# Flamingo layer 0 on one core: the first loads in three groups, and the first maxima on VectorE in a fixed order

## The chip, the core and the metric

The kernel runs on one core of a Trainium2 chip. TensorE (PE) multiplies and transposes, VectorE (DVE), ScalarE (ACT) and GpSimd (POOL) do the rest, and SyncE (SP) issues transfers; ACT and POOL issue transfers too. Each engine works through its own list of instructions in order. The metric is the device time of one execution in microseconds (us).

## The reference

Two layers, each a gated cross-attention-like block and a gated feed-forward block, over `x` of 4 batches of 512 rows by 512:

```python
x = x + tanh(g_xattn[0]) * L0_xattn(layernorm(x), fside, ctx)   # int8 "smooth quant" expert, per batch
x = x + tanh(g_ffn[0])   * L0_ffn(layernorm(x), w_fc, w_proj)   # ternary weights
x = x + tanh(g_xattn[1]) * L1_xattn(layernorm(x), ctx, mask, Wq, Wk, Wv, Wo)   # 16 heads, 8 of keys/values
x = x + tanh(g_ffn[1])   * L1_ffn(layernorm(x), router_w, norm_w, gate_w, up_w, down_w)   # top 2 of 8 experts

def smooth_quant_linear(x, w):          # fside (512 x 512), then ctx (512 x 256), are its weights
    s = sqrt(max(amax_cols(|x|), eps) / max(amax_cols(|w|), eps))
    xq, wq = int8 rounding of x / s and w * s, with a scale per row
    return xq @ wq.T * x_scale * w_scale.T

def ternarize(w):                       # w_fc 1280 x 512 and w_proj 512 x 1280
    m = mean(|w|);  return m * (sign of w where |w| > 0.7 m, else 0)
```

The keys and values of layer 1, `ctx @ Wk` and `ctx @ Wv`, depend on no earlier layer.

## The kernel before

Layer 0 runs batch by batch. `int8_block(b)` normalises `X[b]` (`layer_norm`: statistics on VectorE, a root on ScalarE, four normalisations on ScalarE, line 180). It takes the column maximum of the weight `fside` (`weight_max`: one VectorE reduction, line 259, four transposes on PE, line 264, and a small tail) and those of the normalised rows (`column_max`: per 128 columns four transposes, line 198, and a reduction, line 251). From both come the factors: `up_q` (line 294), its root (`sqrt_of`, lines 151 to 158), and two rows made by transposes (line 204). ScalarE copies one row out (line 300); VectorE divides the rows (line 303) and GpSimd multiplies the weight (line 305). Then row maxima (275), scaling (281), transposed copies to bf16 on ScalarE (283), the products (336), `h` (340), SiLU (341), and the same again with the 256 columns of `ctx` as the weight (`cr`).

`mean_of` adds up absolute values of the two ternary weights on ScalarE (line 395). `w_fc` is held in ten tiles (`hold_rows`), while `w_proj` comes through two staging buffers of tag `t8` (`stage_rows`, line 368). `load_signs` turns both into signs on VectorE (414, 417). `ternary_in` and `ternary_block(b)` are the ternary feed-forward (462, 449).

`keys_values(b)` makes the keys and values of layer 1 ahead of time and fills gaps of PE with them: the context is transposed (495) and copied (496), then 16 products of two matmuls (501) per batch. ScalarE copies each product (503) into one of two staging slots, and SP stores it to DRAM (504). A copy therefore needs the store of two products earlier to have landed. The products use two PSUM banks in turn.

The code is written batch by batch, and a scheduler puts the instructions of each engine in order by priority, which is the order of the code unless `tc.high_priority` says otherwise, and by its own estimate of when things are ready. `tc.keep_in_program_order` pins an instruction, and `tc.add_manual_dep` adds a dependency. What an engine has in its list is fixed before the run.

In the kernel before, the loads at the start are issued without waiting: SP issues `x[0]`, `fside[0]`, the cross rows `cr` and the context of batch 1; ACT issues the context of batch 0, `Wk` and `Wv`; POOL issues the gates and `fside[1]`. The loads of `w_fc` alone have a dependency on `Wv`:

```python
        fs0, cr0 = load_rows(0), load_cross(0)
        ctx0 = load_context(0, nc.scalar)
        ...
        held = hold_rows(w_fc)
        fs1 = load_rows(1, nc.gpsimd)
```

Layer 1 follows: attention over 64 heads in a software pipeline, and the experts.

Of the kernel before, what the change touches and what calls it, by code (L numbers as in the profile page):

```python
# [15 lines left out]
P = 128  # L16
# [41 lines left out]
def kernel(  # L58
# [82 lines left out]
    def acc_tile():  # L141
        sums_in[0] += 1
        return bank(4 + sums_in[0] % 4)

    def small(n, tag):
        return sm.tile([P, n], F32, tag=tag, name=tag)

# [62 lines left out]
    with tc.tile_pool(name="q8", bufs=1) as q8, tc.tile_pool(name="l0", bufs=2) as l0, tc.tile_pool(  # L210
# [29 lines left out]
        def home():  # L240
            mine = HOMES[now[0]]
            return bank(mine[next_of("home", len(mine))])
# [5 lines left out]
        def column_max(src, kt, dst):  # L248

            for i in range(kt):  # L250
                nc.vector.tensor_reduce(
                    dst[:, i : i + 1], transposed(src, i, home()), AX.X, ALU.max, apply_absolute_value=True
                )

        def weight_max(w, kt, tag):

            k = kt * P
            top = rooms[now[0]][0]
            nc.vector.tensor_reduce(
                top[:, :k], w.rearrange("p t k -> p k t"), AX.X, ALU.max, apply_absolute_value=True  # L260
            )
            tp = home()
            for i in range(kt):
                nc.tensor.transpose(tp[:, i * P : (i + 1) * P], top[:, i * P : (i + 1) * P], ident)
            am = q8.tile([P, kt], F32, tag=tag + "_am", name=tag + "_am", bufs=2)
            nc.vector.tensor_reduce(am, tp[:, :k].rearrange("p (k t) -> p k t", t=P), AX.X, ALU.max)
            nc.vector.tensor_scalar_max(am, am, Q_EPS)
            nc.vector.reciprocal(am, am)
            return am

        def quantize(src, kt, dst, tag):
# [12 lines left out]

            return sc

        def smooth_quant(a, w, w_max, kt, tag):


            k = kt * P  # L290
            am = small(kt, tag + "_am")
            column_max(a, kt, am)
            q = small(kt, tag + "_q")
            nc.vector.scalar_tensor_tensor(q, am, Q_EPS, w_max, ALU.max, ALU.mult)
            s = sqrt_of(q, kt, tag + "_s")
            nc.vector.tensor_scalar_max(s, s, Q_EPS)
            rs = small(kt, tag + "_rs")
            nc.vector.reciprocal(rs, s)
            s_row = a_row()
            nc.scalar.copy(s_row[:, :k], row_of(s, kt, home())[:, :k])  # L300
            rs_row = row_of(rs, kt, home())
            for t in range(NT):
                nc.vector.tensor_tensor(a[:, t, :], a[:, t, :], rs_row[:, :k], ALU.mult)
            for t in range(NT):
                nc.gpsimd.tensor_tensor(w[:, t, :], w[:, t, :], s_row[:, :k], ALU.mult)
            aT = q8.tile([P, kt, S], BF16, tag=f"q{kt}", name="aT", bufs=2)
            wT = q8.tile([P, kt, S], BF16, tag=f"q{kt}", name="wT", bufs=2)
            a_sc = quantize(a, kt, aT, tag + "a")
            w_sc = quantize(w, kt, wT, tag + "w")
            w_row = a_row()  # L310
            nc.scalar.copy(w_row, row_of(w_sc, NT, home()))
            return aT, wT, a_sc, w_row

        def load_rows(b, queue=nc.sync):
            fs = row_tiles(b % 2 * 2)
            queue.dma_start(fs, rows(fside[b]))
            if b:
                queue.dma_start(X[b], rows(x[b]))
            return fs

        def load_cross(b):
            cr = place_in(dn, SLOT + 3072, NT * DC).rearrange("p (t k) -> p t k", t=NT)
            nc.sync.dma_start(cr, rows(cvec[b]))
            return cr

        def int8_block(b, fs, cr):
            now[0] = b
            xn = row_tiles(b % 2 * 2 + 1)
            layer_norm(b, xn)
            fs_max = weight_max(fs, KD, "fs")  # L330
            aT, wT, a_sc, w_row = smooth_quant(xn, fs, fs_max, KD, "up")
            act = xn[:, : NT // 2, :].rearrange("p a (b n) -> p (a b) n", n=INNER)
            for t in range(NT):
                ps = home()
                for i in range(KD):
                    nc.tensor.matmul(
                        ps, lhsT=aT[:, i, t * P : (t + 1) * P], rhs=wT[:, i, :], start=(i == 0), stop=(i == KD - 1)
                    )
                h = l0.tile([P, 512], F32, tag="h", name="h")
                nc.vector.scalar_tensor_tensor(h, ps, a_sc[:, t : t + 1], w_row, ALU.mult, ALU.mult)  # L340
                nc.scalar.activation(act[:, t, :], h[:, :INNER], AF.Silu)
                nc.gpsimd.tensor_tensor(act[:, t, :], act[:, t, :], h[:, INNER:], ALU.mult)
            cr_max = weight_max(cr, INNER // P, "cr")
            aT, wT, a_sc, w_row = smooth_quant(act, cr, cr_max, INNER // P, "dn")
            gsc = small(NT, "gsc")
            nc.vector.tensor_scalar(gsc, a_sc, tg_xa0, None, ALU.mult)
            for t in range(NT):
                ps = home()
                for i in range(INNER // P):
                    nc.tensor.matmul(  # L350
                        ps,
                        lhsT=aT[:, i, t * P : (t + 1) * P],
                        rhs=wT[:, i, :],
                        start=(i == 0),
                        stop=(i == INNER // P - 1),
                    )
                y = l0.tile([P, 512], F32, tag="h", name="y")
                nc.vector.scalar_tensor_tensor(y, ps, gsc[:, t : t + 1], w_row, ALU.mult, ALU.mult)
                nc.gpsimd.tensor_tensor(X[b][:, t, :], X[b][:, t, :], y, ALU.add)
# [5 lines left out]

        def stage_rows(src, r, n_cols):
            st = l0.tile([P, HF], F32, tag="t8", name="stage")
            nc.gpsimd.dma_start(st[:, : n_cols * P], src[r * P : (r + 1) * P, :])
            return st[:, : n_cols * P]

        def hold_rows(src):

            loads = [nc.gpsimd.dma_start(X[2], rows(src[: NT * P, :]))]
            held = [X[2][:, r, :] for r in range(NT)]
            for r in range(NT, NH):
                held.append(l0.tile([P, D], F32, tag="hT", name="held", bufs=6))
                loads.append(nc.gpsimd.dma_start(held[-1], src[r * P : (r + 1) * P, :]))
            for load in loads:
                tc.add_manual_dep(
                    load.ins,  # L380
                    wkv_in[-1].ins.name,
                    mybir.DependencyInfo(mybir.DependencyClass.Sync, mybir.DependencyReason.DATA),
                    reason="what the first products read comes first",
                )
            return held

        def mean_of(src, n_rows, n_cols, tag, held=None):

            part = small(n_rows + 1, tag + "_part")
            for r in range(n_rows):  # L390
                if held:
                    st, dst = held[r], l0.tile([P, D], F32, tag="r", name="size")
                else:
                    st = dst = stage_rows(src, r, n_cols)
                nc.scalar.activation(dst, st, AF.Abs, accum_out=part[:, r : r + 1])
            nc.vector.tensor_reduce(part[:, n_rows:], part[:, :n_rows], AX.X, ALU.add)
            ps = turn_bank()
            nc.tensor.matmul(ps[:, 0:1], lhsT=ones, rhs=part[:, n_rows:], start=True, stop=True)
            mean = w0.tile([P, 1], F32, name=tag + "_mean")
            nc.vector.tensor_scalar(mean, ps[:, 0:1], 1.0 / (HF * D), 1e-5, ALU.mult, ALU.max)  # L400
            thr = w0.tile([P, 2], F32, name=tag + "_thr")
            nc.vector.tensor_scalar(thr[:, 0:1], mean, 0.7, None, ALU.mult)
            nc.vector.tensor_scalar(thr[:, 1:2], mean, -0.7, None, ALU.mult)
            return mean, thr
# [112 lines left out]
                        lambda i: wkv[1][:, i, c : c + 512],  # L517
                    )

        fs0, cr0 = load_rows(0), load_cross(0)  # L520
        ctx0 = load_context(0, nc.scalar)
        wkv, wkv_in = [], []
        for w in (wk, wv):
            wkv.append(gu[:, 3 + len(wkv)].rearrange("p k f -> p (k f)").rearrange("p (k n) -> p k n", k=KC))
            wkv_in.append(nc.scalar.dma_start(wkv[-1], w.rearrange("(k p) n -> p k n", p=P)))
        held = hold_rows(w_fc)
        fs1 = load_rows(1, nc.gpsimd)

        def keys_values_of(b):
            places = (7, 3) if b < 2 else (3,)  # L530
# [788 lines left out]
```

## Time and profile before

| | us |
|---|---|
| median of 3 runs | 1573.49 (1570.37 to 1573.74) |
| the profiled execution | 1570.78 |
| its span in the trace | 1569.0 |
| first matmul of a ternary block (L462) | 164.89 |
| attention and experts, in the cut 430 to 1480: PE busy | 1036.84 |

The page of a profile gives busy time by engine, and `PEclk` is the clock that TensorE was granted. In a timeline row the columns are start and length in us, engine, line, operation, what is written and read, the count, and in brackets the idle time of that engine just before and what ended it. Queue q0 holds the loads that POOL issues, q1 those of SP, q10 those of ACT. Lengths and idle times are of one execution.

### The profile page before, as it was taken

To read this page: it belongs to the slowest core of one execution; us is meant where nothing else is said; L and a number is where in the kernel's file an instruction comes from. 1 tells how busy PE (TensorE), PEld (TensorE's weight loads), DVE (VectorE), ACT (ScalarE), POOL (GpSimd) and SP (SyncE) were. 2 spreads that over 40 slices of the span, in tenths; PEclk is the share of its full clock that TensorE was granted. 3 is DMA by queue.
4 is the path that set the end of the run, shared out by engine and by line. 5 is a ranking of instruction groups with operands and counts; after the bars stand their busy time and mean duration, and the time that the engine had idled before them with its cause. 6 is when DMAs were issued, how large, how long until landed. Compare 5 with 4: busy or idle time off the path is not lost. (4 is left out here: it accounts for less than half of the span.)

```text
span 1569.0 us, 15875 instructions
## 1 busy us (share of the span) xinstructions
PE 1476.3 (94%) x4285; PEld 743.3 (47%) x4294; DVE 890.7 (57%) x2311; ACT 565.8 (36%) x1157; POOL 416.2 (27%) x540
## 2 busy tenths in 40 slices
PE   4888898889999999999999999999999998899995
PEld 2444666566544444444444444444444443355563
DVE  5797636556275555586565675665667552653320
ACT  4645554444243332353333353333433331422111
POOL 2232314253311113132131141141141111435422
PEclk9999999999999999999999999999999999999998
DMA  8533101112455455576454485465584653566642
GB/s 311 198 116 133 54 34 67 35 41 81 127 157 147 133 143 149 141 214 157 127 150 138 138 218 158 114 184 145 156 231 128 164 138 97 149 119 150 120 81 38
DMA packets 110840, 211.10 MB, mean 135 GB/s; under 512 B 28816, under 2 KB 32912, under 8 KB 110752
## 3 DMA queue, kind: packets, MB, share of 16 engines
q0 software_dynamic: 32736, 97.73, 23.8%
q1 hardware_dynamic: 70224, 100.74, 22.7%
q10 hardware_dynamic: 7792, 11.60, 2.1%
q8 instruction: 37, 0.61, 0.2%
q14 instruction: 51, 0.42, 0.1%
HBM read 95.34 MB, written 34.93 MB: 83 GB/s over the span
## 5 line engine op out<-in xcount | busy, mean ns | idle before, releaser
L674 DVE CUSTOM_DVE_ANT_0 e<-bank,mask_b 128x512 f32<-128x512 f32 x256 | 175.1, 688 | 245.0 <-PE bank L669 244.9
L669 PE MATMUL bank<-kT,qT 128*128 128x512 f32 x512 | 231.1, 593 | 0.0
L708 PE MATMUL bank<-wo,oT 128*128 128x512 f32 x512 | 230.7, 592 | 0.3 <-ACT oT L698 0.3
L694 PE MATMUL bank<-eT,v 128*128 128x512 f32 x512 | 230.5, 592 | 0.1
L677 ACT ACTIVATE e<-e,nmax 128x512 f32<-128x512 f32 x256 | 184.4, 720 | 79.8 <-DVE nmax L674 73.0
L656 PE MATMUL bank<-gu,wq 128*128 128x512 f32 x384 | 174.9, 594 | 1.2 <-DVE nmax L674 1.2
L571 DVE STREAM_TRANSPOSE blocks<-e 128x512 f32<-128x512 f32 x256 | 158.9, 677 | 28.2 <-DMA eT<-blocks 23.8
L694 PEld LDWEIGHTS bank<-eT,v 128*128 128x128 f32 x512 | 97.1, 190 | 123.4 <-issue 109.8
L669 PEld LDWEIGHTS bank<-kT,qT 128*128 128x128 f32 x512 | 97.0, 190 | 123.1 <-issue 115.0
L708 PEld LDWEIGHTS bank<-wo,oT 128*128 128x128 f32 x512 | 97.1, 190 | 122.7 <-issue 120.3
L698 ACT COPY oT<-bank 128x512 f32<-128x512 f32 x64 | 37.4, 584 | 316.1 <-PE bank L694 298.4
L656 PEld LDWEIGHTS bank<-gu,wq 128*128 128x128 f32 x384 | 72.3, 190 | 91.9 <-issue 82.1
L635 POOL DMA_DIRECT2D wq<-in_L_xattn_Wq_dram x64 | 48.5, 758 | 246.1 <-PE bank L656 223.5
L685 DVE TENSOR_SCALAR e<-e,rt 128x512 f32<-128x512 f32 x256 | 107.9, 484 | 2.1
L650 POOL DMA_DIRECT2D wo<-in_L_xattn_Wo_dram x64 | 36.3, 567 | 268.9 <-PE bank L708 265.7
L660 ACT ACTIVATE qT<-bank 128x512 f32<-128x512 f32 x64 | 38.2, 597 | 171.9 <-PE bank L656 166.0
L462 PE MATMUL bank<-xfT,fcT 128*128 128x512 f32 x320 | 88.9, 411 | 0.0
L449 PE MATMUL bank<-pjT,hT 128*128 128x512 f32 x320 | 86.6, 405 | 0.3 <-DVE hT L474 0.3
L1093 PE MATMUL bank<-gu,turned 128*128 x192 | 86.5, 593 | 0.0
L501 PE MATMUL bank<-dn,gu 128*128 128x512 f32 x128 | 68.7, 659 | 9.9 <-ACT dn L503 4.0
L473 POOL TENSOR_TENSOR r<-r 128x512 f32<-128x512 f32 x40 | 41.7, 1042 | 111.9 <-ACT hT L472 105.4
L1215 PE MATMUL bank<-dn,hidT 128*128 x144 | 69.3, 605 | 1.5 <-DVE hidT L1189 1.5
(360 smaller groups left out, 1885.8 us busy)
## 6 DMA issues: line engine op xcount, KB each, us to landing
eT<-blocks SPq DMA_DIRECT2D x1016, 64.0 KB
wq<-in_L_xattn_Wq_dram POOLq DMA_DIRECT2D x64, 256.0 KB
wo<-in_L_xattn_Wo_dram POOLq DMA_DIRECT2D x64, 256.0 KB
kd<-dn SPq DMA_DIRECT2D x32, 256.0 KB
vd<-dn SPq DMA_DIRECT2D x32, 256.0 KB
kT<-kd POOLq DMA_DIRECT2D x32, 256.0 KB
v<-vd POOLq DMA_DIRECT2D x32, 256.0 KB
turned<-blocks SPq DMA_DIRECT2D x96, 64.0 KB
```

The source lines that it names most:

```text
L449: nc.tensor.matmul(outs[t], lhsT=h[:, t * P : (t + 1) * P], rhs=pjT[:, j, :], start=(j == 0 and u == 0), stop=(j == NH - 1 and u == 1),)
L462: nc.tensor.matmul(ps, lhsT=fcT[:, i, j * P : (j + 1) * P], rhs=xT[u][:, i, :], start=(u == 0 and i == 0), stop=(u == 1 and i == KD - 1),)
L571: nc.vector.transpose(blocks[:, :, :, t, :].rearrange("p c s r -> p s c r"), src.rearrange("p (s c i) -> p s c i", c=NQ, i=Q))
L656: nc.tensor.matmul(ps, lhsT=th[:, i, :], rhs=xT[:, :, i, :], start=(i == 0), stop=(i == KD - 1))
L669: nc.tensor.matmul(ps, lhsT=qT[:, t * P : (t + 1) * P], rhs=kT, start=True, stop=True)
L674: nc.vector.tensor_tensor_reduce(e, ps, mask_b[b], -1.0, 3.0e38, ALU.add, ALU.min, nmax[:, t : t + 1])
L677: nc.scalar.activation(e, e, AF.Exp, bias=nmax[:, t : t + 1], scale=-1.0, accum_out=total[:, t : t + 1])
L685: nc.vector.tensor_scalar(es[:, t, :], es[:, t, :], rt[:, t : t + 1], None, ALU.mult)
L694: nc.tensor.matmul(ps, lhsT=v[:, s, :], rhs=eT[:, :, s, :], start=(s == 0), stop=(s == NT - 1))
L708: nc.tensor.matmul(sums[b][t], lhsT=oT[:, t * P : (t + 1) * P], rhs=to, start=(n == 0), stop=(n == NHEAD - 1))
L1093: nc.tensor.matmul(ps, lhsT=xgT[k], rhs=gu[:, bass.ds(e, 1), k, :], start=(k == 0), stop=(k == KD - 1))
L1215: nc.tensor.matmul(ps, lhsT=hT[f], rhs=dn[:, bass.ds(e, 1), f, :], start=(f == 0), stop=(f == NF - 1))
```

## The change

1. The loads at the start come in three groups. First `x[0]`, the contexts of batches 0 and 1, and the left half of `Wk`'s columns. Once that half has landed, SP issues `fside[0]`, the right half of `Wk` and `Wv`. Once `Wv` has landed, SP issues the cross rows, and POOL issues `w_fc`, `fside[1]` and `x[1]`; the `w_proj` tiles have a dependency on `Wv` too. `Wk`'s second half and `Wv` move from ACT's queue to SP's.
2. In block 0 the maximum of `fside` is taken after the column maxima of the rows (`w_max` is a function that is called then), and block 0's weight maxima are pinned in program order.
3. The absolute values of both ternary weights start only when block 0's factor row has been copied (`factors[0]`).

```diff
+    def after(ins, first, reason):
+        tc.add_manual_dep(ins.ins, first.ins.name, ...)
...
-            nc.vector.tensor_reduce(
+            largest = nc.vector.tensor_reduce(
                 top[:, :k], w.rearrange("p t k -> p k t"), AX.X, ALU.max, apply_absolute_value=True
             )
+            if not now[0]:
+                tc.keep_in_program_order(largest)
...
             column_max(a, kt, am)
+            if callable(w_max):
+                w_max = w_max()
...
-            nc.scalar.copy(s_row[:, :k], row_of(s, kt, home())[:, :k])
+            made = nc.scalar.copy(s_row[:, :k], row_of(s, kt, home())[:, :k])
+            factors.append(made)
...
-            fs_max = weight_max(fs, KD, "fs")
+
+            fs_max = weight_max(fs, KD, "fs") if b else lambda: weight_max(fs, KD, "fs")
...
-            nc.gpsimd.dma_start(st[:, : n_cols * P], src[r * P : (r + 1) * P, :])
+            after(nc.gpsimd.dma_start(st[:, : n_cols * P], src[r * P : (r + 1) * P, :]), wkv_in[-1], FIRST)
...
-                nc.scalar.activation(dst, st, AF.Abs, accum_out=part[:, r : r + 1])
+                size = nc.scalar.activation(dst, st, AF.Abs, accum_out=part[:, r : r + 1])
+                if r == 0:
+                    after(size, factors[0], "the first block's factors come first")
...
-        fs0, cr0 = load_rows(0), load_cross(0)
         ctx0 = load_context(0, nc.scalar)
...
+        wkv_in = []
+        half = NKV * HD // 2
+        for i, c, n in ((0, 0, half), (0, half, half), (1, 0, 2 * half)):
+            queue = nc.sync if wkv_in else nc.scalar
+            w = (wk, wv)[i][:, c : c + n]
+            wkv_in.append(queue.dma_start(wkv[i][:, :, c : c + n], w.rearrange("(k p) n -> p k n", p=P)))
+            if len(wkv_in) == 1:
+                fs0 = load_rows(0, first=wkv_in[0])
+            else:
+                after(wkv_in[-1], wkv_in[0], FIRST)
+        cr0 = load_cross(0, wkv_in[-1])
         held = hold_rows(w_fc)
-        fs1 = load_rows(1, nc.gpsimd)
+        fs1 = load_rows(1, nc.gpsimd, wkv_in[-1])
```

The scheduler's order on each engine changes with it through layer 0. On ScalarE seven product copies (503) stand before the first factor row's copy (300), where two stood; on POOL the first `w_proj` load comes after the multiplication of the weight (305), where it came before. The amount of arithmetic is the same.

## The prediction

> **What bounds the kernel now.** I read the busy table first, then the table by stages, the waits of the opening, the timeline from 17 to 63 us, and last the DMA queues in cuts of a few microseconds.
>
> Busy time and stages (columns: stretch, its length, busy us of PE, PEld, DVE, ACT and POOL with counts, granted clock, DMA share, GB/s):
>
> ```profile
> PE 1476.3 (94%) x4285; PEld 743.3 (47%) x4294; DVE 890.7 (57%) x2311; ACT 565.8 (36%) x1157; POOL 416.2 (27%) x540
> 0.00:21.25 21.25, 3.99 (x11) 2.08 (x11) 6.80 (x13) 3.94 (x6) 4.74 (x14) 1.00 0.93 324
> 21.25:45.00 23.75, 20.64 (x63) 10.60 (x64) 18.27 (x32) 15.56 (x35) 9.95 (x22) 0.93 0.72 260
> 63.00:100.00 37.00, 30.88 (x156) 16.77 (x156) 32.51 (x65) 22.07 (x40) 12.37 (x12) 1.00 0.40 141
> 100.00:140.00 40.00, 37.04 (x159) 19.51 (x159) 36.48 (x78) 21.32 (x42) 10.49 (x12) 0.96 0.39 138
> ```
>
> TensorE bounds the whole, and after 215 us (1036.8 of 1050 us busy in attention) nothing can absorb or add time. So the change is worth what it does to the moment when the first ternary block starts, 164.9 us. Up to there TensorE loses 17.3 us in the first 21.25, and from 63 to 140 VectorE is as full as TensorE: 69.0 of 77 us. An early gain must pass through VectorE.
>
> The opening's waits of TensorE (us, times, longest), and the timeline's rows that the change touches:
>
> ```profile
> PE bank L495 <- DMA dn<-in_ctx_dram: 10.0, 1, 10.0
> PE bank L501 <- DMA gu<-in_L_xattn_Wk_dram: 3.9, 1, 3.9
> PE bank L264 <- DVE dn L259: 3.4, 1, 3.4
> 17.57 3.62 DVE L259 TENSOR_REDUCE dn<-gu 128x512 f32<-128x2048 f32 x1 [5.93 <-DMA gu<-in_fside_BxS2xS_dram]
> 22.31 2.93 ACT L180 ACTIVATE gu<-gu,ln_d,ln_rstd 128x512 f32<-128x512 f32 x4 [7.96 <-DVE ln_d L176]
> 31.92 0.16 DVE L294 SCALAR_TENSOR_TENSOR up_q<-up_am,fs_am 128x4 f32<-128x4 f32 x1
> 33.17 0.20 ACT L151 ACTIVATE up_s_y<-up_q 128x4 f32<-128x4 f32 x1
> 35.19 0.58 ACT L300 COPY dn<-bank 128x512 f32<-128x512 f32 x1
> 35.85 4.95 POOL L305 TENSOR_TENSOR gu<-gu,dn 128x512 f32<-128x512 f32 x4 [9.31 <-ACT dn L300]
> 54.49 0.58 ACT L503 COPY dn<-bank 128x512 f32<-128x512 f32 x1 [3.85 <-DMA kd<-dn]
> ```
>
> VectorE sits behind `fside` until 17.57 with the finished statistics of `x` queued behind that reduction, so the normalised rows come at 22.31 and the factors' square root at 33.17. The last row is the warning: a copy of a key product sat until the store of two products earlier had landed, because the staging has two slots. The DMA queues (packets, MB, share) from 25 to 29 us and from 29 to 32 us show why; the first store was issued at 25.73:
>
> ```profile
> q0 software_dynamic: 442, 1.44, 98.9%
> ...
> q0 software_dynamic: 234, 0.93, 76.4%
> q1 hardware_dynamic: 146, 0.27, 23.4%
> ```
>
> Beside GpSimd's loads (q0) not one packet of the store (q1) moved for over 3 us; its 0.26 MB were through only at 32, 6.3 us after issue. The store behind the row at 54.49 was issued at 47.95: 6.5 us.
>
> **The first group.** `x[0]` 1.05, two contexts 0.52 each, half of `Wk` 0.52: 2.62 MB. The cuts of before add up to 2.34 MB by 10 us and 0.43 in the next, so 2.62 MB are in by 10.7; with 0.6 for the end I take 11.3. The context lands first as before (9.9). Key products start at 11.3, not 15.83: TensorE's wait of 3.9 goes.
>
> **The second group** is issued on SP once that half has landed: `fside`, the rest of `Wk`, `Wv`, 2.62 MB. The gate costs a gap: the load issued at 67.50 with empty queues moved 0 GB/s in its first half microsecond, 63 and 203 in the next two, then about 400. I take 1.7 us and 0.39 MB/us: `fside` lands at 16.3 (before 17.57), `Wv` at 20.3 (19.41). What is queued behind SP's second wait (on `Wv`) is the cross rows and then every key store; on POOL the `w_fc` loads wait for `Wv` too.
>
> [...]
>
> **The fixed order on VectorE.** Statistics no longer wait behind the weight maximum: shift and scale are ready near 13.1. ScalarE still has its table load for the gates (12.85 to 14.35 before), then normalises to 17.3. Four column maxima of 0.68, two of them after a bank comes free, end at 20.6; the weight maximum, 3.7, at 24.3 (before 21.2); its transposes and tail 2.0: `up_q` at 26.3 instead of 31.92. So far 5.6 us are won. The two other first maxima (cross rows 1.94, second `fside` 3.7) move later, without changing VectorE's total.
>
> **What ScalarE does with it.** In the changed program five product copies stand ahead of the factors' table load and square root, and two more ahead of the copy of the factors' row (L300); before, it was none and none after the first two. Copies 3 to 7 need stores 1 to 5 landed. Copies 1 and 2 end by 18.5. SP can issue store 1 only after its wait on `Wv`, at 20.9, with the cross rows (512 packets of 1 KB) ahead in the ring. They move 0.3 MB before GpSimd's loads arrive, the rest at the 60 packets per us that q1 got in 30 to 33, until 26.1; then the store's 128 packets until 28.2, landed 28.7. Copy 3 ends 29.3; store 3 is issued.
> - Slow end, 6.3 us as in the row: copy 5 ends 36.2, table load 1.28, root at 37.7; GpSimd's 4.7 MB run dry near 37, so store 5 takes 3.4 and L300 ends at 40.8.
> - Middle, 4.0 us since it follows store 2 in a busy ring: root 35.5, L300 ends 39.1.
> - Fast end, at most 2.85 (the copies at 106.03 and 109.46 are two stores apart with no load beside): store 1 at 24.3, root 29.9, L300 ends 32.4.
>
> I take 40.0 against 35.77, nearer the loaded row because 4.7 MB of GpSimd loads are in flight: 4.2 us late, the 5.6 us lost in ScalarE's queue. The ten absolute values of `w_fc`, which the change holds back until after L300, cost nothing: they end at 46.2, under GpSimd's multiplication.
>
> **What follows.** The first `w_proj` load moves on POOL from ahead of the multiplication L305 to behind it: 40.0 + 5.0 = 45.0, and 5.3 to land (40.75 issued, 46.09 used): 50.3. Then on ScalarE two absolute values of 1.27 and two copies of 0.58 to 54.0; two pairs of transposed copies (1.09) and a copy to 56.8; the third staged tile (issued 51.6 + 5.3) to 58.2, a pair to 59.3, the fourth to 60.6, the last pair to 61.7 against 60.56. The first `h` (62.86) comes 1.0 late. By then VectorE has not run what it had before: the cross maximum 1.94, one sign step 0.46 and eight tiny ones of about 0.12, 3.4 us. From 63 to 140 it has 8 us idle, mostly waits inside the same chain; I let it absorb 1.0. Sum: 1.0 + 3.4 − 1.0 = 3.4 us at the ternary block. TensorE has one more key product done by then, in gaps, which I cost at nothing: the chain and not the filling is late; if filling set the end it would give back 1.0.
>
> The profiled execution took 1570.78 (span 1569.0 and 1.8 around it): 1574.2. The median of the runs shown, 1573.49, is 2.7 above it: 1576.9. Ends: stores at the fast end bring the first `h` some 4 us earlier, less 3.4 of VectorE's work; stores slower still (7 us, and the staged tiles late with them) make it 8.
>
> **Rivals.**
> - *Faster.* One mechanism: stores land within about 3.5 us of issue although loads are in flight, since group three is smaller than what was in flight before. Then the root comes near 30, and TensorE keeps the 3.9 of the `Wk` wait and about 1 of the 3.4 behind the weight maximum: 4.9, so 1568.6. For it: `up_q` is really 5.6 us earlier. Against: 6.3 and 6.5 us in the only two loaded cases.
> - *No change.* ScalarE's late start is made good in the 8 + 6.9 us that VectorE idles from 63 to 165 (the latter in 140 to 165): 0 to 1.5, 1574.2. Against: the idle there ends on POOL's scaling and ScalarE's rows of the same chain.
> - *It does not do what it says.* The half of `Wk` lands no earlier than 14, because context and `x` already fill the engines until then: 2 us of gap are paid and nothing is won; 1 to 2 us slower than the forecast, inside its range.
>
> **The numbers.** Forecast 0.58, faster 0.28, no change 0.14 (the last rival lies within the first). A measurement of this kernel can tell about 0.2%, 3.1 us. The forecast's spread puts 0.50 beyond that and 0.08 within; faster gives 0.26 and 0.02; no change 0.10 within and 0.02 on each side. Faster 0.28, same 0.20, slower 0.52. Range: from 1567.5, a little past the faster rival, to 1582, the slow end; the forecast's own range is 1574 to 1582.
>
> **What would show it.** Right: the first key product near 11, `up_q` near 26, ScalarE idle for some 10 us until a `kd` store ends it, the root after 35, the first `xfT` product near 168. Wrong: the third copy before 26, or the root before 32; then the end is early. If the root is late and the ternary block still starts by 165, it was the absorbing.

## The result, and the profile after

| | us |
|---|---|
| median of 8 runs, changed kernel | 1579.51 (1574.63 to 1585.65) |
| median of 8 runs, kernel before | 1572.32 (1566.23 to 1575.21) |
| ratio | 1.0056, 95% interval 1.0039 to 1.0073 |
| profiled execution after / its span | 1581.88 / 1580.1 |
| the same ratio in a later session, on another chip (e9) | 1.0071, 95% interval 1.0044 to 1.0097 |

The change makes the kernel slower, by 0.56% or some 9 us, where 3.4 us were forecast. The line of busy times and the table by stages after (columns as in the prediction: stretch, its length, busy us of PE, PEld, DVE, ACT and POOL, granted clock, DMA share, GB/s):

```profile
PE 1483.4 (94%) x4285; PEld 746.4 (47%) x4294; DVE 887.4 (56%) x2311; ACT 565.0 (36%) x1157; POOL 415.1 (26%) x540
0.00:21.25 21.25, 10.54 (x35) 6.15 (x36) 6.01 (x20) 7.81 (x12) 3.12 (x19) 1.00 0.75 247
21.25:45.00 23.75, 15.51 (x42) 6.39 (x40) 14.31 (x19) 8.38 (x19) 8.46 (x12) 0.93 0.80 298
63.00:100.00 37.00, 31.26 (x161) 17.84 (x163) 31.69 (x79) 24.09 (x46) 7.18 (x10) 1.00 0.49 171
```

TensorE is 6.5 us ahead at 21.25 (10.54 busy instead of 3.99) and has given 5.1 of it back by 45 (15.51 instead of 20.64). So the early start is real, and most of it is lost in the second stage. The timeline rows that answer to those of before:

```profile
14.51 2.92 ACT L188 ACTIVATE gu<-gu,ln_d,ln_rstd 128x512 f32<-128x512 f32 x4
21.86 3.64 DVE L267 TENSOR_REDUCE dn<-gu 128x512 f32<-128x2048 f32 x1
25.59 0.59 ACT L522 COPY dn<-bank 128x512 f32<-128x512 f32 x1 [6.08 <-DMA kd<-dn]
31.12 0.59 ACT L522 COPY dn<-bank 128x512 f32<-128x512 f32 x1 [4.94 <-DMA kd<-dn]
29.48 0.16 DVE L308 SCALAR_TENSOR_TENSOR up_q<-up_am,fs_am 128x4 f32<-128x4 f32 x1
34.70 0.20 ACT L159 ACTIVATE up_s_y<-up_q 128x4 f32<-128x4 f32 x1
40.91 0.59 ACT L314 COPY dn<-bank 128x512 f32<-128x512 f32 x1
41.59 4.97 POOL L320 TENSOR_TENSOR gu<-gu,dn 128x512 f32<-128x512 f32 x4 [10.74 <-ACT dn L314]
```

The factors `up_q` are ready 2.4 us earlier than before (29.48 instead of 31.92), the root comes 1.5 later and GpSimd's multiplication 5.7 later (41.59 instead of 35.85). In between ScalarE stands still in front of product copies (L522) whose slot is not free. The waits of TensorE up to 60 us and those of ScalarE up to 165 (us in all, times, longest) say the same:

```profile
PE bank L520 <- ACT dn L522: 10.6, 4, 4.3
```

```profile
ACT dn L522 <- DMA kd<-dn: 18.9, 6, 6.1
ACT dn L522 <- DMA vd<-dn: 7.4, 3, 3.4
```

Before, ScalarE waited for one store, 3.8 us; now for nine, 26.3 us. The waits of TensorE for `Wk` (3.9) and for the weight maximum (3.4) are gone, and four waits for ScalarE's copies, 10.6 us, have taken their place. From 25 to 29 us the queues (packets, MB, share) were:

```profile
q0 software_dynamic: 300, 1.16, 83.4%
q1 hardware_dynamic: 146, 0.26, 16.7%
```

The stores (q1) do get packets here beside GpSimd's loads (q0), where before not one moved, but few: the store issued in that stretch landed 6.5 us after its issue, and the one issued at 21.60, the second, after 9.4 us. With no load beside them the stores issued at 88.10 and 90.65 landed after 2.0 us.

From there on the chain stays late and gets later. Marks in us, and in the last two columns all the time that TensorE waited, and that it was busy, up to the first attention matmul. The last row is e9, a second execution of the changed kernel, on another chip:

| | first key product | root | multiplication | first `h` | second `up_q` | ternary block | first `Wq` matmul | waiting | busy |
|---|---|---|---|---|---|---|---|---|---|
| before | 15.83 | 33.17 | 35.85 | 62.86 | 79.25 | 164.89 | 413.5 | 59.7 | 353.8 |
| after | 12.65 | 34.70 | 41.59 | 67.08 | 87.24 | 172.59 | 424.6 | 61.1 | 363.5 |
| after, e9 | 12.65 | 34.68 | 41.16 | 66.21 | 87.27 | 170.10 | 422.1 | 59.9 | 362.2 |

Marks of the same kernel differ by up to 2.5 us between the two executions. From the first `Wq` matmul to the end, before and after take 1155.5 us each. So the whole difference of their spans, 11.1, arises before it; but TensorE's waiting grew by only 1.4 us there. It is the busy time that grew, by 9.7 (8.4 in e9), with four more records of product matmuls (0.43 each, 1.7 us) behind it. The other 8.0 us are nearly all the same matmuls at a slower clock. Stretches of the table by windows, after and then before (columns: stretch, length, PE busy and in the second fence the other engines, clock, DMA share, GB/s):

```profile
26.00:31.00 5.00, 3.78 (x8) 0.66 1.01 391
47.00:55.00 8.00, 6.71 (x10) 0.57 0.85 248
115.00:120.00 5.00, 3.90 (x15) 0.66 0.02 8
143.00:154.00 11.00, 9.61 (x23) 0.53 0.06 24
201.00:206.00 5.00, 5.00 (x21) 0.66 0.00 0
```

```profile
26.00:31.00 5.00, 4.88 (x26) 2.98 (x26) 4.91 (x7) 3.40 (x10) 0.54 (x1) 1.00 1.00 378
47.00:55.00 8.00, 4.45 (x21) 2.49 (x20) 5.46 (x17) 4.15 (x10) 1.06 (x2) 1.00 0.74 254
36.00:40.50 4.50, 3.58 (x7) 1.79 (x8) 2.18 (x5) 2.69 (x7) 4.50 (x4) 0.62 0.30 117
57.00:61.00 4.00, 4.00 (x18) 2.90 (x17) 2.67 (x9) 3.51 (x9) 0.53 (x1) 0.58 0.50 139
101.00:106.00 5.00, 5.00 (x11) 2.13 (x10) 3.86 (x7) 0.59 (x1) 4.66 (x4) 0.66 0.14 54
```

Up to 420 us both traces record a granted clock of either 1.00 or, for 3.41 us or a multiple of it (6.83, 10.24), 0.50. Half of these stretches' length is 8.5 us before and 18.8 after, the latter 1.2% of the 1580 us. The records begin only at 26.2 us before and at 16.9 after, and for the time ahead of them the views print 1.00. But TensorE ran at half speed there too: in the kernel before, the two records of one product matmul take 1.92 us at 24.07 and 1.02 us at 26.53; in the changed kernel six such records take 4.93 us at 12.65 and two 1.02 us at 17.86. By an estimate that counts half of TensorE's busy time in all these stretches, the opening's included, half speed cost 12.8 us before, 20.2 after and 19.0 in e9, up to the first `Wq` matmul. (The opening has 4.5 of it before and 3.1 after, where the records begin 9.3 us earlier.)

After, each of the eight stretches up to 420 us begins in a wait of TensorE of 2.0 us or more, or within 2 us behind it; the first five belong to the waits that end at 26.2 (2.51 us), 48.3 (4.28), 115.5 (2.64), 142.5 (2.50) and 199.9 (2.24). Behind the first 16 us and up to 420, before has six waits of 2.0 us or more and after has ten. It is no fixed rule: after, the waits that end at 39.2 (2.08) and 80.0 (2.89) have no half clock behind them, and before, the stretch at 36.4 lies at waits of 1.66 and 1.33 only. One and the same wait, 2.71 us for VectorE's scaling near 340 us, stands in ten of the fourteen traces and has half clock behind it in seven of them (in the changed kernel, where it ends at 348.13 and the stretch begins at 347.98; not in before, where it ends at 338.61, nor in e4 and e10).

The mean clock of the whole execution was 0.980 to 0.984 in the eight runs after, and 0.985 to 0.990 in the 35 runs of the kernel before that accompanied the first four experiments. Within those 35, nine runs at 0.989 or more took 1566.3 us on average, nine at 0.986 or less 1572.5. From these means a thousandth of clock is worth an estimated 1.5 to 2 us, and a thousandth of TensorE's 1480 busy us is 1.5; the 0.0055 between the means of the two kernels are 8 us, nearly the whole result. (These means count the opening, which has no records, as full speed.)

### The profile page after: what moved, and what is told of

Its sections match the earlier page's. It is cut to its first block, busy times and chain, and to the rows that moved or that the text cites. A ratio compares the mean times of both kernels' runs of the same rounds, so it can differ in the third digit from the quotient of the medians.

```text
span 1580.1 us, 15884 instructions
## 1 busy us (share of the span) xinstructions
PE 1483.4 (94%) x4285; PEld 746.4 (47%) x4294; DVE 887.4 (56%) x2311; ACT 565.0 (36%) x1157; POOL 415.1 (26%) x540
## 5 line engine op out<-in xcount | busy, mean ns | idle before, releaser
L598 DVE STREAM_TRANSPOSE blocks<-e 128x512 f32<-128x512 f32 x256 | 159.0, 678 | 27.1 <-DMA eT<-blocks 22.0
L712 DVE TENSOR_SCALAR e<-e,rt 128x512 f32<-128x512 f32 x256 | 108.3, 486 | 2.1
L687 ACT ACTIVATE qT<-bank 128x512 f32<-128x512 f32 x64 | 38.2, 597 | 172.6 <-PE bank L683 166.6
L520 PE MATMUL bank<-dn,gu 128*128 128x512 f32 x128 | 71.0, 678 | 13.9 <-ACT dn L522 10.6
L520 PE MATMUL bank<-gu,dn 128*128 128x512 f32 x128 | 67.5, 643 | 5.7 <-ACT dn L522 5.5
```

Of the source, the lines that this page charges most:

```text
L520: nc.tensor.matmul(ps, lhsT=lhs(i), rhs=rhs(i), start=(i == 0), stop=(i == KC - 1))
L598: nc.vector.transpose(blocks[:, :, :, t, :].rearrange("p c s r -> p s c r"), src.rearrange("p (s c i) -> p s c i", c=NQ, i=Q))
L712: nc.vector.tensor_scalar(es[:, t, :], es[:, t, :], rt[:, t : t + 1], None, ALU.mult)
```

## The experiments

Two theories stood against each other. *ScalarE's queue*: product copies that need a store landed stand ahead of the chain, and everything later follows from that. *The pinned order*: VectorE's postponed maxima are what makes it late. From the fifth run on a third was tested, *the clock*. The order of instructions on the engines is fixed when the kernel is built, and an edit anywhere can move instructions elsewhere; where that matters it is said. Times on marks are of one execution each, ratios of all.

All results together; ratios are to the kernel before on the same chip, waiting is TensorE's up to the ternary block, clock is the mean of the runs.

| kernel | ratio (95%) | clock | root | ternary block | waiting |
|---|---|---|---|---|---|
| before | 1 | 0.987 | 33.2 | 164.9 | 39.9 |
| after | 1.0056 (1.0039 to 1.0073) | 0.982 | 34.7 | 172.6 | 40.6 |
| e1 root first | 1.0043 (1.0022 to 1.0063) | 0.982 | 27.9 | 157.1 | 38.8 |
| e2 four slots | 0.9978 (0.9960 to 0.9996) | 0.985 | 29.3 | 157.2 | 33.1 |
| e3 order alone | 1.0016 (0.9997 to 1.0035) | 0.983 | 34.8 | 163.7 | 34.9 |
| e4 loads alone | 0.9998 (0.9979 to 1.0018) | 0.987 | 33.9 | 159.0 | 38.8 |
| e5 more work | 1.0023 (1.0003 to 1.0044) | 0.988 | 34.5 | 164.5 | 33.8 |
| e6 slots, before | 1.0005 (0.9989 to 1.0021) | 0.987 | 33.1 | 160.3 | 37.3 |
| e7 no hold | 1.0033 (1.0017 to 1.0049) | 0.981 | 34.1 | 171.6 | 39.6 |
| e8 loads and slots | 0.9975 (0.9959 to 0.9991) | 0.987 | 29.9 | 150.0 | 31.4 |
| e9 after again | 1.0071 (1.0044 to 1.0097) | 0.982 | 34.7 | 170.1 | 39.5 |
| e10 half the work | 0.9984 (0.9968 to 1.0000) | 0.988 | 34.8 | 160.5 | 31.1 |
| e11 work, before | 1.0093 (1.0066 to 1.0121) | 0.990 | 33.7 | 164.8 | 38.1 |
| e12 best and work | 1.0037 (1.0022 to 1.0052) | 0.987 | 29.5 | 157.4 | 30.0 |

### e1: the root first

```diff
-                nc.scalar.copy(st, ps)
+                copied = nc.scalar.copy(st, ps)
+                products.append(copied)
+                if 2 < len(products) <= 16:
+                    after(copied, factors[0], "the first block's factors come first")
```

> The change, but every key and value product copy of batch 0 from the third on is held behind the factors' row on ScalarE. Theory A (ScalarE's queue): the wait on key stores ahead of the root is what costs. Then up_q comes near 27, the root near 27.5 (34.7 in the change), the row's copy ends near 30, the first h comes at 55 to 59 (67.1), the ternary block starts at 161 to 166 (172.6), and the time is 0.995 to 1.001 of the kernel before. Theory B (the later loads): w_fc, the second fside, x[1] and w_proj come later whatever ScalarE does. Then the root is early too, but h stays at 64 or later and the ternary block at 169 or later: 1.003 to 1.006.

The chain does what ScalarE's queue says: `up_q` at 27.75, root at 27.94, ternary block at 157.08, 15.5 us earlier than in the changed kernel and 7.8 earlier than before. The end does not follow: 1576.92, still 0.43% slower than before. The held copies hold the products too. At the first `Wq` matmul 212 of the product matmuls' records have started, 228 before; the other 16 (6.9 us) come later, with 4.9 us of waiting from there to the hundredth score matmul (2.0 before). And the clock is as low as after: one wait of 8.99 us that ends at 40.2, and half clock from 27.7 to 44.7. So an early ternary block is worth nothing by itself here.

### e2: four staging slots

```diff
-                st = place_in(dn, SLOT + 2048 + 512 * next_of("kvs", 2), 512)
+                places4 = (2048, 2560, 0, 512) if b == 0 else (2048, 2560)
+                st = place_in(dn, SLOT + places4[next_of("kvs", len(places4))], 512)
```

> The change with four staging slots for batch 0's products instead of two, so a copy waits for the store of four products earlier; the order on ScalarE stays. The second pair lies where batch 1's context went, so that context (0.52 MB) leaves the first group of loads. Theory A: copies 3 and 4 go at once, copy 5 waits for store 1 (25.6 in the change), so the root comes near 28 to 29, the row near 32, h at 58 to 63, 1.000 to 1.003 of the kernel before. Theory B: h at 65 or later, 1.004 or more, as the change.

The two more slots lie where the context of batch 1 was put, which is loaded later, so that the first group is 0.52 MB smaller. All lists but SP's keep their order through the opening. Later TensorE's differs from 66.8 us of the changed kernel on, ScalarE's from 79.9, where batch 1's normalisation goes ahead of copies, and GpSimd's from 102.1 (see e10). 1566.31, faster than the changed kernel and than the kernel before. Not one wait for a store is left among ScalarE's longest seven up to 165 us; for copies it now waits only where TensorE has not finished the product:

```profile
ACT dn L523 <- PE bank L520: 27.5, 17, 3.3
```

So the change without the store waits is not slower. Whether the waits or the order behind the opening made the difference this run alone doesn't tell.

### e3 and e4: one part alone

e3 is the kernel before with the late, pinned weight maximum; e4 is the changed kernel without it and without the hold on the absolute values.

```diff
 e3, in the kernel before:
+            if not now[0]:
+                tc.keep_in_program_order(largest)
...
-            fs_max = weight_max(fs, KD, "fs")
+            fs_max = weight_max(fs, KD, "fs") if b else lambda: weight_max(fs, KD, "fs")
 e4, in the changed kernel:
-            if not now[0]:
-                tc.keep_in_program_order(largest)
...
-            fs_max = weight_max(fs, KD, "fs") if b else lambda: weight_max(fs, KD, "fs")
+            fs_max = weight_max(fs, KD, "fs")
...
-                if r == 0:
-                    after(size, factors[0], "the first block's factors come first")
```

> The kernel before with VectorE's order alone: the fside maximum of block 0 after the column maxima, maxima of block 0 pinned; loads and absolute values as before. In its list ScalarE has the ten absolute values of w_fc and one product copy ahead of the root, and two w_proj absolute values ahead of the factors' row. Theory A: up_q is early (27 or so) and this doesn't help, the root comes at 36 or later and the row at 48 or later; 1.003 to 1.010. Theory B: VectorE's order is the good part of the change and the loads are the bad one: 0.996 to 1.000.

> The change without VectorE's order and without the hold on the absolute values: the three groups of loads alone. ScalarE has three copies and one absolute value ahead of the root, so one wait on a store instead of three. Theory A: the root comes at 31 to 33.5, the row at 36 to 38, h at 62 to 65, 1.000 to 1.003. Theory B: late loads cost as in the change, h at 66 or later, 1.004 to 1.007.

1571.03 and 1569.67: neither part alone can be told from the kernel before. Both have less TensorE waiting (34.9 and 38.8 instead of 39.9), but the pinned order has the low clock, 0.983, and the loads alone have not, 0.987. Both missed their expectations in the marks: e3's `up_q` came at 33.15, not near 27, with a ratio between the two theories', and e4's first `h` at 59.48, before 62. The whole change has the waiting of neither. So neither of these two parts alone makes the whole loss, and the two together make most of it (e7, without the third part, has 1.0033). What they do to each other these runs don't show.

### e5: needless work in TensorE's waits

```diff
+                nth = next_of("nth", 999)
+                again = 2 if b == 0 and 8 <= nth < 16 else 0
+                for _ in range(again):
+                    nc.tensor.matmul(ps, lhsT=lhs(0), rhs=rhs(0), start=True, stop=True)
                 for i in range(KC):
```

> The changed kernel, with the first matmul of products 9 to 16 of batch 0 done three times instead of once (sixteen needless matmuls, 0.43 us each at full clock, 6.9 us of TensorE's time; the result does not change). Clock theory: what the change costs is not TensorE's waiting (40.6 us up to the ternary block, before 39.9) but the half clock that follows each wait of about 2 us or more; needless work that fills the wait of 4.28 us at 44 us takes away the half clock behind it. Then the mean granted clock rises by 0.002 or more from 0.982, and the time falls by 2 to 4 us although there is 6.9 us more to do: about 1576 beside 1579. Rival one, TensorE's work is the bound and the clock is chance: 6.9 us slower, 1586. Rival two, ScalarE's queue is the bound and TensorE's work is hidden: no change, 1579, clock 0.982.

The expectation has the size of the work wrong: the trace shows each of these matmuls as two records of 0.43 us, so that 16 are 13.8 us and not 6.9 (the same holds for e10 to e12: 8 are 6.9, 12 are 10.3). With 13.8 us more to do the kernel is faster than the changed one: 1.0023 against 1.0056 and, on another chip, 1.0071. The opening is that of the changed kernel (root 34.47, multiplication 40.61), the mean clock is 0.988 instead of 0.982, and up to the ternary block no stretch of half clock is left at all. Its waits of 2.06, 2.21 and 2.48 us, ended at 26.2, 59.2 and 111.0, have none behind them. The work also moved ScalarE's list, from 54.3 us of the changed kernel on, and GpSimd's, from 102.1 on; so this run alone doesn't tell needless work from a new order. e10 has less of the work.

### e6: four slots without the change

The edit of e2 in the kernel before.

> The kernel before, with four staging slots for the products of batch 0 instead of two (ScalarE's list stays the same, its product copies wait for the store of four products earlier). If the slots alone made the changed kernel with four slots faster than before (waits of TensorE up to the ternary block 33.1 instead of 39.9), this comes 5 us or more below before, 1564. If slots pay only where the change has put five product copies ahead of the square root, which the list here has not, it is within 2 us of before, 1568 to 1571, with the square root at 33 as before, and clock 0.987.

1573.06, no difference, root at 33.09. The gain of e2 is not that of the slots alone. That they pay where copies stand ahead of the chain fits this, but is argued.

### e7: the change without its third part

```diff
-                if r == 0:
-                    after(size, factors[0], "the first block's factors come first")
```

> The changed kernel without its third part: absolute values of the ternary weights do not wait for the first factor row. ScalarE's list then has three product copies and five absolute values ahead of the square root, where the changed kernel has five copies, and no copy between root and row copy, where it has two. ScalarE's queue theory: root near 30 to 34, row copy right behind it, GpSimd's multiplication near 36 instead of 41.59; TensorE's waits up to the ternary block 36 to 39. Clock: if the pinned order of the maxima lowers it by itself (0.983 with that alone, 0.987 in the kernel before and with the loads alone), it stays near 0.983 and the time is 1572 to 1576; if the store waits of the product copies lower it, it rises to 0.986 and the time is 1568 to 1571.

1577.76: still slower, clock 0.981. Copies ahead of the square root are three instead of five, the multiplication starts at 37.22 instead of 41.59, and yet the ternary block starts at 171.58. So the hold is at most a part of the cause (the intervals overlap), and lateness at 40 us is not what decides. The time lies outside both ranges of the expectation; the clock stayed low, as it foresaw for a pinned order that lowers it by itself.

### e8: loads in groups and four slots

e4 and e2 together.

> The three groups of loads without the pinned maxima and without the hold, with four staging slots for batch 0. Adding up: the loads alone had 38.8 us of TensorE waits up to the ternary block and clock 0.987; four slots took 7.5 us of waits off the changed kernel. If the two add, waits of 32 to 34, clock 0.987 and 1563 to 1565, 5 us below before and the fastest of all. If the slots paid only for copies that stood in front of the square root (three here), it is like the loads alone: 1568 to 1570.

1567.92, ratio 0.9975: with e2 the fastest against before, though not the 1563 to 1565 of adding up. Waiting is 31.4 as expected.

### e9 to e12: half the work, and needless work elsewhere

e9 is the changed kernel again. e10 is e5 with `again = 1`; e11 is the edit of e5 in the kernel before; e12 is e8 with it for products 5 to 10.

> The changed kernel itself, beside the three below and the kernel before on one chip, so that they can be compared directly. Both theories: 1.0056 of the time of before, about 1580, mean granted clock 0.982 against 0.987.

> The changed kernel with the first matmul of products 9 to 16 of batch 0 done twice (eight needless matmuls, 3.4 us at full clock; three times each gave 1575.2, clock 0.988). ScalarE's list differs from that of the changed kernel by one later product copy only. Clock theory: the clock rises about half as much, to 0.985, and the time stays below that of the changed kernel, 1576 to 1579. If instead the gain came from the five later copies that ScalarE's list had at another place with sixteen matmuls: clock 0.982 and 1580 to 1583.

> The kernel before with the same sixteen needless matmuls, 6.9 us. Its products stand in the way of no store wait of more than 3.8 us, and it has five or six waits of 2 us or more up to 420 us where the changed kernel has ten. Clock theory: the clock rises by at most 0.002 (3 us), so that 4 to 7 us of the needless work remain: 1575 to 1579, ratio 1.002 to 1.0045. If needless work helps any kernel by the same 0.006 of clock: 1569 to 1571, no slower than before.

> Three groups of loads and four slots without the pinned maxima and the hold (1567.9), with twelve needless matmuls in products 5 to 10 of batch 0 (5.2 us), meant for its longest remaining wait, 4.39 us at 36.7. Its clock is 0.987 already and it has three waits of 2 us or more. Clock theory: the half clock behind that wait goes (0.002, 3 us) and the needless work is nearly hidden in it: 1566 to 1569, no clear difference. If every needless matmul counts: 1573.

e10 missed its expectation on the good side: 1563.63, 14.3 us less than the changed kernel on the same chip (1577.93) with 6.9 us more to do. Its opening is as late as ever: root 34.84, multiplication 41.09, and ScalarE waits as long for the keys' stores, 18.1 us in six times. What it no longer has is the 7.4 us of waits for the values' stores. Of the spans' difference to e9, 13.4 us, 1.6 are busy time (6.9 of work, less 8.5 by the clock) and 11.8 are waiting, 6.9 of it at most filled by the work. The rest, some 5 us, would be order. GpSimd's long rows of batch 1 in the changed kernel and then in e10:

```profile
100.88 1.27 POOL L320 TENSOR_TENSOR gu<-gu,xlast 128x512 f32<-128x512 f32 x1 [9.02 <-ACT xlast L314]
102.11 2.50 POOL L381 TENSOR_TENSOR gu<-gu,y 128x512 f32<-128x512 f32 x2
104.57 3.72 POOL L320 TENSOR_TENSOR gu<-gu,xlast 128x512 f32<-128x512 f32 x3
```

```profile
94.51 5.14 POOL L320 TENSOR_TENSOR gu<-gu,xlast 128x512 f32<-128x512 f32 x4 [6.18 <-ACT xlast L314]
99.62 4.95 POOL L381 TENSOR_TENSOR gu<-gu,y 128x512 f32<-128x512 f32 x4
```

In the changed kernel two additions of `y` to `X[0]` stand inside the multiplication of batch 1's weight, which ends at 108.3 instead of 99.7; in e10 they follow it. The changed kernel (after and e9) is the only one of all with that multiplication in two pieces. And ScalarE's rows just before, in the changed kernel and then in e10:

```profile
74.89 0.59 ACT L522 COPY dn<-bank 128x512 f32<-128x512 f32 x1 [1.98 <-DMA vd<-dn]
79.41 0.59 ACT L522 COPY dn<-bank 128x512 f32<-128x512 f32 x1 [3.44 <-DMA vd<-dn]
80.37 2.93 ACT L188 ACTIVATE dn<-gu,ln_d,ln_rstd 128x512 f32<-128x512 f32 x4
```

```profile
71.60 0.59 ACT L526 COPY dn<-bank 128x512 f32<-128x512 f32 x1 [1.35 <-issue]
72.40 2.93 ACT L188 ACTIVATE dn<-gu,ln_d,ln_rstd 128x512 f32<-128x512 f32 x4 [0.22 <-DVE ln_d L184]
```

Batch 1's normalisation (L188) waits in the changed kernel for VectorE's last statistics step (78.93, behind the `fside` maximum of 3.67) and then for two copies, one of them held 3.44 us by a store; in e10 it runs at 72.40. Second `up_q` 87.24 against 82.75, second `h` 128.05 against 117.26, ternary block 172.59 against 160.51.

But e7 speaks against this order as what decides. There the multiplication is in one piece too, from 88.70 to 93.66, batch 1's normalisation begins at 68.81 and the second `up_q` comes at 82.31, all as early as in e10 or earlier; and yet its ternary block starts at 171.58 and the kernel is 0.33% slower than before. What e7 shares with the changed kernel and not with e10 is the clock: from 95 us to the ternary block both have 13.7 us of half clock (6.8 in e9), e10 none, and they wait 12.2 us there against 6.5.

e11 missed on the other side: 1581.11, 13.6 us slower than before. The clock rose as expected, to 0.990 (by 0.002, 3 us), but all of the 13.8 us of work remains and 3 more: here the needless matmuls displaced useful products, of which 52 records instead of 28 come behind the first `Wq` matmul. e12 is 9.7 us slower than e8 by the ratios (1.0037 against 0.9975, of 1567.5), of 10.3 us of work: the clock theory's 1566 to 1569 was missed, and the other case, 1573, was met. The wait that the work was meant for did shrink, from 4.39 to 1.73 us, but the clock stayed at 0.987. So needless work is not good in itself. Time fell only in the changed kernel, where the longest wait of the opening, 4.28 us, became 1.80 in e5 and 3.62 in e10; and in both the order behind the opening changed with it. What filling a wait is worth without a new order no run shows.

What stays open: whether every stretch of half clock is owed to the wait in front of it. The count of waits of 2.0 us or more goes with the mean clock in most kernels (ten, ten and nine in after, e9 and e7 at 0.981 to 0.982; three to six in before, e4, e5, e6, e8, e10 at 0.987 to 0.988), but not in all (six in e1, one of them of 8.99 us, at 0.982; six in e11 at 0.990). All kernels with a clock of 0.981 to 0.983 have the pinned order (after and e9, e1, e3, e7); but e2, e5 and e10 have it too, at 0.985 to 0.988. Whether it is this order that lowers the clock no run isolated. And e10's other order came about by accident; no run changed that order alone, so that its part, some 5 us of waiting, is argued from the rows, with e7 against it.

## Why the prediction was right, and where it was not

The sign and the range were right. The mechanism in the opening was seen as forecast: early factors, lost again in ScalarE's queue behind stores. But that this lateness sets the end was not borne out: e10 has all of it and ends no later than the kernel before. TensorE's slower clock, which the prediction did not have, makes up most of the result, and why these kernels have more of it stays open. That the sign came out right is thus partly luck. Step by step:

- **First group.** The half of `Wk` was in at 11.3, as forecast (SP's next load goes out at 11.31). The 0.6 us for the end were the author's estimate: the group's last packet ended at 11.01. The first key product came at 12.65, for it waited 1.22 us more for ScalarE's copy of the transposed context, which the sum did not have; TensorE is still 6.5 us ahead at 21.25. The rival that the change does not do what it says is out.
- **Second group.** The load issued at 67.50 was misread: in the trace nothing moves for 1.0 us, then 127, 156 and 250 GB/s in the next three half microseconds, and about 400 from 70.0. `fside` landed at 16.8 (16.3). The cross rows went out at 20.58, the first store at 21.07, as forecast (20.3 and 20.9).
- **Order on VectorE.** Normalised rows end at 17.4 (17.3), the weight maximum runs 21.86 to 25.5 (20.6 to 24.3), but `up_q` came at 29.48 and not 26.3. The step failed on TensorE: the transposes of that maximum (L274, 27.24) stand in its list behind a product that waited 2.51 us for the third copy. The forecast had followed ScalarE's list behind the stores and not TensorE's.
- **Stores.** The third copy ran at 25.59, earlier than 29.3 and, by 0.4 us, than the mark that was to say "wrong" and that the end is early; the end was late all the same, so this mark did not tell. The first store landed after 4.4 us. The second, issued 0.5 us behind it, was the slow one, 9.4, which moved the fourth copy to 31.12; the third took 6.5. Root 34.70 (35.5 to 37.7), row copy ended 41.5 (40.0, ends 39.1 to 40.8): ScalarE's loss at the multiplication was 5.7 us against 4.2.
- **First `h`.** The term "1.0 late" measured 4.2. Two more store waits of 1.84 and 1.99 us on ScalarE, ended at 54.3 and 59.9 among the transposed copies, were not in the sum; `w_proj` itself was used at 51.1 (50.3).
- **VectorE's work not yet done.** Forecast 3.4; from first `h` to the second `up_q` the changed kernel loses 3.8 more, with the cross maximum, 1.94, in the rows at 71.84 and the statistics behind the next maximum. Of the right size, and the 1.0 to be absorbed was 0.3: 7.7 at the ternary block instead of 3.4. But e10 also runs its cross maximum behind the first `h` (69.64) and still starts that block 4.4 us earlier than before. So a loss up to the second `up_q` can be won back behind it; e10, 3.5 us late there, won back 7.9, the changed kernel 0.3.
- **The ternary block as the measure.** The step that "the change is worth what it does to the moment when the first ternary block starts" is refuted. e1 starts it 7.8 us early and ends 0.43% late, with product work left over; and from that block to the first `Wq` matmul the changed kernel lost another 3.4 us, by the clock (half of the half-clock stretches' length there is 3.4 before, 6.8 after). Two more of these stretches lie behind 215 us, where "nothing can absorb or add time".
- **The clock.** It was in no term of the sum. It is the part of the result that waiting does not explain: 1.4 us more of waiting, 7.5 us more of half speed.

The faster rival's condition, stores within 3.5 us, did not hold. The first five needed 4.4, 9.4, 6.5, 6.7 and 6.9, which the trace's row for a loaded store, 6.3, was near; the stores at 88.10 and 90.65, with no load beside them, landed after 2.0 us.

## What to carry to other kernels

Split an engine's time into work, waiting and slow clock before you say what a change costs: here TensorE waited hardly longer (1.4 us), in more pieces of 2 us and more (ten instead of six), and paid at half clock (20.2 us instead of 12.8 by the estimate above), mostly behind them. Before a copy is moved ahead in an engine's list, count its staging slots and the landing time of their stores beside the traffic of that moment (here two slots, and 4.4 to 9.4 us); with two more slots, and the order that came with them, this loss became a gain of 0.22%. And a mark early in the kernel measures an edit only as long as the same amount of filling work lies behind it: e1 started its ternary block 7.8 us early with 6.9 us of products left over, and ended 0.43% late.

## What the runs showed of the hardware

In the changed kernel the first five stores, of 256 KB each, landed 4.4 to 9.4 us after issue beside GpSimd's loads, and those at 88.10 and 90.65 after 2.0 us without them; two of ScalarE's waits for the early ones were of 4.94 and 6.08 us. TensorE's granted clock fell to half there, for 3.41 us or multiples, in or within 2 us behind eight of ten waits of 2.03 to 4.28 us; one wait, of 2.71 us, had half clock behind it in seven traces of ten. In the 11 us from 143, which hold the longest stretch (10.24 us), TensorE was busy for 9.61. In the opening TensorE ran at half speed, by the length of its product matmuls, until records of the clock begin, at 26.2 us before and 16.9 after; the clock column prints 1.00 for it. Programs with 13.8 and 6.9 us of needless matmuls, and the new order that came with them, were some 5 and 14 us faster than the changed kernel (e5, e10); elsewhere such work cost nearly its length (9.7 us of 10.3 in e12, 13.6 of 13.8 in e11).
